# A two-layer transformer on one core: K and Q of layer 1 in one pass, the softmax division after P V, the row maximum fused

## The chip, the cores and the metric

The kernel runs on one core of a Trainium2 chip. The metric is the device time of one execution in microseconds. The core has five engines that run side by side and meet through semaphores: TensorE (PE in the profile, with PEld for its weight loads), VectorE (DVE), ScalarE (ACT), GpSimd (POOL) and SyncE (SP), which here issues all DMAs from a single queue. Each engine does its instructions in the order in which they were issued.

## The reference

Input is x of 2 batches x 512 positions x 512 features, in fp32. Two layers follow, each an attention and a feed-forward, each with a layer norm in front and a layer norm of its result before it is added to x:

```
x = x + LN(attention0(LN(x)))     32 heads of 128, 8 key/value heads, rotary, causal
x = x + LN(ffn0(LN(x)))           x W^T + bias, with 8 low-rank pairs
x = x + LN(attention1(LN(x)))     32 heads of 128, biases, not causal
x = x + LN(ffn1(LN(x)))           silu(h1) * h3 through 1376, with low-rank pairs
```

Attention of layer 1, which most of the change is about, is for each head

```
q = rmsnorm(x Wq + bq) * gq ;  k = rmsnorm(x Wk + bk) * gk ;  v = x Wv + bv
attn = softmax(q k^T / sqrt(128)) ;  out = concat(attn v) Wo + bo
```

## The kernel before, in words

All products are exact to about fp32: an operand is split into hi + lo[...], and `mm3` (line 393) issues hi hi, hi lo and lo hi. So every operand costs a cast to hi (often ScalarE) and a subtraction for lo (GpSimd or VectorE). `pick` (127) chooses for such an operation the engine that the planner expects to be done first.

The program is straight-line. A planner in Python lays out the order of issue: pieces of TensorE's work are `Item`s with a condition, and each has stages, written as generators, for the other engines and DMAs. `streams` (345) merges the main stream (scores and P V products) with fills (projections "q", V "v", output projections "o"), each placed at a nominal position in the main stream and let in when its condition holds. The planner keeps a clock of its own from a table of costs; `PHASES` (37) holds numbers of buffers and weights for six stages of the work. Large tiles share an arena of 37 slots of 128x1024 fp32 (`arena_t`, 230), where `NBUF` (171) limits each kind: in phases 3 and 4, which cover layer 1's attention, two "nat" tiles may live. What the planner decided is fixed: on the chip each engine follows that order and waits for what it needs.

A unit is a pair of heads of one batch; a layer has 32 units, in order, batch by batch for a few weights at a time. In layer 1, `l1_weights` (1020) loads K and Q weights of a pair in two halves each, split on the way, with two bias broadcasts. `proj` (1039) makes K, then Q: for 128 positions, 12 matmuls with x stationary and 256 weight columns moving. Two such results fill a PSUM bank (512 columns), then VectorE adds the bias into a tile "nat", ScalarE squares, VectorE sums, GpSimd raises to -1/2. K is multiplied by its row factors; Q's factors are kept for the softmax. `flip` (1097) transposes 32x32 blocks on VectorE, stores them to DRAM (kdk, kdq) and loads them back with the blocks in place, and splits them.

`l1_score` (1169) makes 128x512 scores in a bank (ps_s). VectorE takes the negated row maximum (`tensor_reduce`) and multiplies it by Q's row factor (mr); ScalarE's exp takes factor and maximum as scale and bias. `softmax_tail` (681), which layer 0 uses too, then divides: reciprocal of the row sum on VectorE, and a multiplication of P by `mul` on any of three engines. Layer 0's scores already have mask and maximum in one VectorE instruction (989).

In 110 of the 128 heads (flag "lag": 50 in layer 0, 60 in layer 1) P is transposed as K and Q are: blocks on VectorE (tile T), a store to pd or pc and four loads (PT), then the split into "pt" tiles. The P V products of such a head (`av_items`, 839) run during the next head: O^T accumulates in a bank ps_oy, ScalarE casts it to hi (with V's bias in layer 1), VectorE subtracts for lo, both from PSUM. `out_proj` (617) multiplies by Wo into ps_oy, and VectorE adds to y. The other 18 heads transpose P on TensorE (`pv_items`, 767).

Of the kernel before, what the change touches and what calls it, by code (L numbers as in the profile page):

```python
# [30 lines left out]
LAT = 0.1  # L31
FIRST = "x0 x1 x2 k x3 q r v y o z"
# [24 lines left out]
class Item:  # L57
    """a piece of TensorE's work, to be issued when cond holds"""
# [5 lines left out]
class Engine:  # L64
    """An engine that keeps its order of issue, with a clock (us) of its work."""
# [58 lines left out]
class Engines:  # L124
    WEIGHT = dict(vector=1.0, scalar=0.5, gpsimd=0.0)

    def pick(self, *cands):
        """issue the one of the candidates (engine, op, args...) that is done first"""
# [21 lines left out]
    def mul(self, out, a, s):  # L150
        """by a factor of each row"""
        self.pick(("gpsimd", "tensor_scalar", out, a, s, 1.0, ALU.mult, ALU.mult),
                  ("vector", "tensor_scalar", out, a, s, None, ALU.mult),
                  ("scalar", "activation", out, a, AF.Copy, dict(scale=s)))

    def copy(self, out, a):
        """from PSUM"""
        self.pick(("scalar", "copy", out, a), ("vector", "tensor_copy", out, a))
# [8 lines left out]
class Kern:  # L167
    """Work is written as items: functions, or generators that yield the time
    (of TensorE's work) after which their next stage is to be issued."""

    NBUF = dict(TN=1, KT=2, W=14, Wk=4, raw=3, bb=2, bqk=1, nat=2, qk=10, v=4, P=7, x=8, xn=2, pt=5, T=4, PT=3, ot=6, tmp=2, A=5,
                v32=2, q32=4, k32=3, p32=1,
                m=6, mr=6, rs=6, ri=6, st=6, mv=10, ve=8, r=10, c=8, r8=6, rq=4,
# [43 lines left out]
    # the large tiles: a half or the whole of a slot each (halves of one type only in a slot)  # L217
    HALF = dict(W=2, Wk=1, nat=2, v=2, PT=2, TN=2, KT=2, raw=1, bb=1, bqk=1, qk=1, P=1, x=1, A=1, T=1, xn=1, pt=1, ot=1,
# [77 lines left out]
    def phase(self, i):  # L296
        """what is tuned for each phase of the work"""
# [27 lines left out]
    def wait(self, tag, n=1):  # L325
        """in a stage: until n slots are free, first come first served"""
# [7 lines left out]
    def low(self, eng):  # L334
        """in a stage of low priority: until the engine has nothing issued to it"""
# [9 lines left out]
    def streams(self, main, fills, bg):  # L345
        """Issue the streams of items, each in its order: a fill when its nominal place in
        main has come, or main waits; bg starts at its nominal place."""
# [30 lines left out]
    def pe(self, t):  # L378
        """t: at the full clock, which TensorE has after a busy tick only"""
# [13 lines left out]
    def mm3(self, out, pairs, start=True, stop=True):  # L393
        """exact hi/lo products: hi hi + hi lo + lo hi"""
# [11 lines left out]
    def setup(self):  # L406
# [11 lines left out]
        self.pd = [self.dr.tile([P, 2, 4, 256], F32, name=f"pd{i}") for i in range(3)]  # L418
        self.kd = {n: [self.dr.tile([P, 4, 256], F32, name=f"kd{n}{i}") for i in range(2)] for n in "kq"}
        self.ready = {}  # L420
        self.ident = cp.tile([P, P], F32, name="ident")
# [7 lines left out]
    def consts(self):  # L429
# [5 lines left out]
        nc.vector.scalar_tensor_tensor(self.g, self.gqk[:, 0:1], SCALE, self.gqk[:, 1:2], ALU.mult, ALU.mult)  # L435
# [6 lines left out]
    def split(self, hi, lo, raw):  # L442
        """hi + lo = raw exactly"""
# [105 lines left out]
    def resid(self, b, tt, lvl):  # L549
        """x of level lvl + 1 = x + LN(y); returned short of a constant of each row"""  # L550
# [10 lines left out]
        if lvl == 3:  # L561
# [10 lines left out]
            nc.sync.dma_start(self.xsrc(b, tt, 4), x)  # L572
            self.rel(x)
# [6 lines left out]
        def store():  # L580
# [8 lines left out]
            nc.sync.dma_start(self.xsrc(b, tt, lvl + 1), xo)  # L589
            self.rel(xo)  # L590
# [3 lines left out]
    def boundary(self, b, tt, lvl):  # L594
        """from the finished y of level lvl on"""
# [21 lines left out]
    def out_proj(self, b, first, last, ot, w, badd, lvl):  # L617
        """y += O Wo over the heads of this unit"""
# [62 lines left out]
    def softmax_tail(self, st, j, qt, ps, bias, scale, w):  # L681
# [3 lines left out]
        rs = self.t("rs", [P, 1])  # L685
        nc.scalar.activation(pr[:, :w], ps[:, :w], AF.Exp, bias=bias, scale=scale, accum_out=rs)
        yield
        self.rel(bias, ps)
        ri = self.t("ri", [P, 1])
        nc.vector.reciprocal(ri, rs)  # L690
        yield
        nc.mul(pr[:, :w], pr[:, :w], ri)
        yield
        self.rel(rs, ri)
        if not st.get("lag"):
            st["p", j, qt] = pr
            return
        # P^T = 32 x 32 blocks transposed on VectorE, and the blocks put in place on their way through DRAM
# [19 lines left out]
        if ("T", j, qt ^ 1) not in st:  # L718
            return
        yield from self.wait("PT")  # L720
# [5 lines left out]
        for kc in ((1, 0), (0, 2, 3, 1))[h] if st["causal"] else range(NT):  # L726
# [21 lines left out]
            else:  # L748
                yield from self.wait("pt")
                hl = self.t("pt", [P, 2, 256], F32R)  # L750
                hi, lo = hl[:, 0, :], hl[:, 1, :]
            hi, lo = (x.rearrange(v, a=4, q=32) for x in (hi, lo))
# [6 lines left out]

    def unit_done(self, st):  # L760
        """after the last use of V"""
# [5 lines left out]
    def pv_items(self, st, j, voff, causal, bias):  # L767
        """transposes of P, then O^T = V^T P^T, split"""
        box = {}

        def tr(kc):
# [5 lines left out]
            if kc == NT - 1:  # L777
                self.rel(*[st["p", j, qt] for qt in range(NT)])
            n = S - q0 * P
# [59 lines left out]
    def av_items(self, st, j, voff, bias):  # L839
        """O^T = V^T P^T by halves of the queries, split"""  # L840
# [4 lines left out]
        def av(h, kc):  # L845
# [17 lines left out]
            if j == 1:  # L863
                self.unit_done(st)
            oh = self.t("ot", [P, S], F32R)
            ol = self.t("ot", [P, S], F32R)
# [816 lines left out]
```

## Time and profile before

| | |
|---|---|
| median of 3 runs | 2111.77 us (2107.32 to 2115.55) |
| the profiled execution: span, the only time that the page gives of it | 2117.8 us |
| TensorE busy | 2056.7 us, 97% |
| VectorE busy | 1801.4 us, 85% |
| GpSimd busy | 1446.3 us, 68% |
| ScalarE busy | 1337.7 us, 63% |
| DMA engines, mean busy share by the queue of SP | 60.9% |

The page gives the busy time of each engine, the granted clock of TensorE, and groups of instructions by operation and tile. Since every instruction goes through one helper, all have line 102, and a group is known by its tiles: ps_pj are projections, ps_s scores, ps_oy P V products and output projections, "ar" any tile of the arena. A matmul's own duration overlaps the next one's, so matmuls are timed by the pieces of a chain. Stages by time: start to about 700 us is layer 0's attention, its feed-forward runs between 640 and 800, layer 1's attention goes on to about 1890, and then comes layer 1's feed-forward. The median of the timed runs lies 6.0 us below the span of the profiled execution.

### The profile page before, as it was taken

The page shows a single profiled execution, that of the slowest core. Times are in us where ns is not written, and L with a number is a line of the kernel's source. Part 1 is how long each engine was busy: PE and PEld are TensorE (multiplying, and loading weights), DVE is VectorE, ACT ScalarE, POOL GpSimd, SP SyncE. Part 2 cuts the span into 40 slices and gives each one's busy share as a digit, 9 for nine tenths or more (in the row PEclk, how much of TensorE's full clock was granted, in tenths as well). Part 3 has the DMA queues.
Part 4 walks back from the last instruction along what each step waited for, and adds up shares of the span by engine and source line. Part 5 has one row for each costly group of instructions (what it writes and reads, how often), then busy time and mean ns, then how long its engine had stood idle before and what let it go on. Part 6 is the DMA issues. An engine that isn't in the chain of part 4 may idle for free.

```text
span 2117.8 us, 41211 instructions
## 1 busy us (share of the span) xinstructions
PE 2056.7 (97%) x12605; PEld 1827.5 (86%) x12605; DVE 1801.4 (85%) x4210; ACT 1337.7 (63%) x3247; POOL 1446.3 (68%) x1786
## 2 busy tenths in 40 slices
PE   8999999999999999999999999999999999989998
PEld 7888888888888798889899999999999898977886
DVE  7998899899888889889889999899989988888534
ACT  5776677577766668776666666666667666664212
POOL 5686678688875567877677777777777776774212
PEclk9999999999999999999999999999999999999999
DMA  2476567577652235887877777777777787763021
GB/s 98 127 183 166 145 185 183 143 200 199 177 159 66 71 103 166 244 232 223 227 202 229 220 227 211 207 221 219 225 206 232 213 240 212 224 178 93 31 67 44
DMA packets 476566, 370.54 MB, mean 175 GB/s; under 512 B 117400, under 2 KB 424488, under 8 KB 476344
## 3 DMA queue, kind: packets, MB, share of 16 engines
q1 hardware_dynamic: 476344, 367.91, 60.9%
q8 instruction: 99, 1.62, 0.3%
q14 instruction: 123, 1.01, 0.2%
HBM read 232.12 MB, written 135.66 MB: 174 GB/s over the span
## 4 chain that ended last, share of the span: by engine, by line
PE 54%; DMA 12%; DVE 9%; SPq 3%; issue 2%; POOL 2%; ACT 2%; DVEq 0%; ACTq 0%; POOLq 0%
PE ps_pj L102 23%; PE ps_oy L102 19%; PE ps_s L102 10%; DVE ar L102 6%; SPq L102 3%; DMA pd<-ar 3%; DMA ar<-pd 2%; POOL ar L102 2%; DMA kdk<-ar 2%; ACT ar L102 2%; DMA ar<-kdq 2%; DMA kdq<-ar 2%; PE ps_tr L102 1%; DMA ar<-pc 1%; DVE m L102 1%
## 5 line engine op out<-in xcount | busy, mean ns | idle before, releaser
L102 POOL TENSOR_TENSOR ar<-ar,ar 128x256 fp32r<-128x256 f32 (+4 forms) x1223 | 1058.3, 887 | 456.6 <-ACT ar L102 333.6
L102 PE MATMUL ps_oy<-ar,ar 128*128 128x256 f32 (+2 forms) x4014 | 832.2, 342 | 28.7 <-DVE ar L102 14.0
L102 PEld LDWEIGHTS ps_oy<-ar,ar 128*128 128x128 f32 x4014 | 653.5, 190 | 133.1 <-DVE ar L102 22.5
L102 ACT CAST ar<-ar 128x256 fp32r<-128x256 f32 (+3 forms) x1166 | 531.5, 490 | 305.4 <-DMA ar<-pd 117.1
L102 PE MATMUL ps_pj<-ar,xh 128*128 128x256 f32 (+1 forms) x3392 | 635.2, 285 | 0.9 <-POOL ar L102 0.6
L102 PEld LDWEIGHTS ps_pj<-ar,xh 128*128 128x128 f32 x3392 | 536.0, 190 | 14.5 <-POOL ar L102 1.1
L102 PE MATMUL ps_pj<-ar,xl 128*128 128x256 f32 (+1 forms) x1696 | 482.9, 285 | 0.0
L102 DVE STREAM_TRANSPOSE ar<-ar 128x256 f32<-128x256 f32 (+3 forms) x688 | 347.9, 533 | 16.9 <-DMA pd<-ar 9.7
L102 DVE TENSOR_TENSOR ar<-ps_pj,ar 128x512 f32<-128x512 f32 (+2 forms) x448 | 305.4, 683 | 52.5 <-PE ps_pj L102 44.8
L102 PE MATMUL ps_s<-ar,ar 128*128 128x512 f32 (+2 forms) x1252 | 338.5, 376 | 8.6 <-DVE ar L102 4.7
L102 PEld LDWEIGHTS ps_pj<-ar,xl 128*128 128x128 f32 x1696 | 322.9, 190 | 2.1 <-DVE xl L102 0.7
L102 PE MATMUL ps_pj<-xh,ar 128*128 128x512 f32 x816 | 286.6, 399 | 0.7 <-ACT xh L102 0.7
L102 DVE TENSOR_TENSOR y<-ps_oy,y 128x512 f32<-128x512 f32 x272 | 184.8, 680 | 81.8 <-PE ps_oy L102 80.2
L102 PEld LDWEIGHTS ps_s<-ar,ar 128*128 128x128 f32 x1252 | 214.5, 189 | 44.0 <-DVE ar L102 12.6
L102 DVE TENSOR_TENSOR ar<-ar,ar 128x256 fp32r<-128x256 f32 (+5 forms) x328 | 207.9, 652 | 51.1 <-ACT ar L102 50.1
L102 ACT ACTIVATE ar<-ps_s,mr,rq 128x512 f32<-128x512 f32 x256 | 198.6, 777 | 46.7 <-DVE mr L102 36.9
L102 PEld LDWEIGHTS ps_pj<-xh,ar 128*128 128x128 f32 x816 | 154.0, 189 | 31.7 <-ACT xh L102 1.1
L102 DVE TENSOR_REDUCE m<-ps_s 128x1 f32<-128x512 f32 x256 | 170.9, 673 | 6.2 <-PE ps_s L102 5.0
L102 ACT ACTIVATE ar<-ar,ri 128x512 f32<-128x512 f32 (+3 forms) x245 | 149.6, 621 | 38.3 <-DVE ri L102 37.1
L102 POOL TENSOR_SCALAR ar<-ar,ri 128x512 f32<-128x512 f32 (+3 forms) x202 | 133.0, 661 | 54.3 <-DVE ri L102 48.9
L102 PE MATMUL ps_pj<-xl,ar 128*128 128x512 f32 (+1 forms) x408 | 161.2, 395 | 0.0
L102 ACT ACTIVATE ar<-ps_s,m 128x512 f32<-128x512 f32 (+3 forms) x256 | 133.8, 526 | 23.4 <-DVE m L102 14.8
(91 smaller groups left out, 2105.5 us busy)
## 6 DMA issues: line engine op xcount, KB each, us to landing
pd<-ar SPq DMA_DIRECT2D x240, 256.0 KB, 3.7
ar<-pd SPq DMA_DIRECT2D x480, 128.0 KB, 3.3
ar<-pc SPq DMA_DIRECT2D x200, 128.0 KB, 3.0
ar<-in_wq SPq DMA_DIRECT2D x86, 256.0 KB, 4.1
ar<-in_wo SPq DMA_DIRECT2D x86, 256.0 KB, 3.6
kdk<-ar SPq DMA_DIRECT2D x31, 512.0 KB, 4.8
ar<-kdk SPq DMA_DIRECT2D x124, 128.0 KB, 4.0
kdq<-ar SPq DMA_DIRECT2D x31, 512.0 KB, 5.1
```

The costliest lines, as they stand in the source:

```text
L102: r = self.k.tc.keep_in_program_order(f(*args, **kw))
```

## The change

K and Q weights of a pair are laid side by side in one array, loaded in four quarters of 512 columns, and `proj` makes K and Q for 128 positions in one chain of 12 matmuls of 512 columns. Row factors are made per two positions' tiles, for K and Q together. Both nat tiles are taken at once. The projections of layer 1 get a nominal place half a head earlier (EARLY).

In heads with "lag" P is no longer divided. The row sums of the four query tiles gather in one 128x4 tile; `row_factors` takes its reciprocal, stores it to DRAM (rd) and loads it back as R, the 512 factors along the free axis in every partition. When O^T is complete, VectorE multiplies it by R from PSUM into a tile "ob", and the split reads that. A counter `turn` lets the transposes of layer 1's heads take their buffers in the order of heads.

In layer 1 the scores come negated (the factor g has the sign), and one `tensor_scalar` multiplies them by Q's row factor, in place in PSUM, and takes the row minimum; exp then has scale -1.

The rest of the diff: numbers of buffers for the new tiles, a planner stage between a store of x and the release of its tile, and comments taken out.

```diff
-                m=6, mr=6, rs=6, ri=6, st=6, mv=10, ve=8, r=10, c=8, r8=6, rq=4,
+                R=2, ob=1, rs4=3, ri4=2, v32=2, q32=4, k32=3, p32=1,
+                m=6, mr=6, rs=6, ri=6, st=6, mv=10, ve=8, r=10, c=8, r8=6, rq=8,
...
-        nc.vector.scalar_tensor_tensor(self.g, self.gqk[:, 0:1], SCALE, self.gqk[:, 1:2], ALU.mult, ALU.mult)
+        nc.vector.scalar_tensor_tensor(self.g, self.gqk[:, 0:1], -SCALE, self.gqk[:, 1:2], ALU.mult, ALU.mult)
...
@@ softmax_tail
+        if st.get("lag"):
+            if ("rs", j) not in st:
+                st["rs", j] = [self.t("rs4", [P, NT]), 0]
+            rs = st["rs", j][0]
+            nc.scalar.activation(pr[:, :w], ps[:, :w], AF.Exp, bias=bias, scale=scale, accum_out=rs[:, qt:qt + 1])
+            yield
+            self.rel(bias, ps)
+            st["rs", j][1] += 1
+            if st["rs", j][1] == NT:
+                self.spawn(lambda: self.row_factors(st, j, rs))
...
+        head = st["head", j]
+        while not st["causal"] and self.turn < head - 2:
+            yield 0.1
...
+        while not st["causal"] and self.turn < head:
+            yield 0.1
         yield from self.wait("PT")
...
+    def row_factors(self, st, j, rs):
+        nc = self.nc
+        ri = self.t("ri4", [P, NT])
+        nc.vector.reciprocal(ri, rs)
+        yield
+        self.rel(rs)
+        d = self.rd[st["slot", j]]
+        nc.sync.dma_start(d, ri)
+        yield
+        self.rel(ri)
+        yield from self.wait("R")
+        R = self.t("R", [P, S])
+        nc.sync.dma_start(R, d.rearrange("(o p) t -> o (p t)", o=1).broadcast_to([P, S]))
+        yield
+        st["R", j] = R
...
@@ av_items
+            yield from self.wait("ob")
+            t = self.t("ob", [P, S])
+            R = st["R", j]
+            nc.vector.tensor_tensor(t.rearrange("m (t p) -> m t p", t=NT), po.rearrange("m (t p) -> m t p", t=NT),
+                                    R.rearrange("m (p t) -> m t p", t=NT), ALU.mult)
...
-                nc.scalar.copy(oh, po)
-                yield
-                nc.vector.tensor_tensor(ol, po, oh.bitcast(F32), ALU.subtract)
+                nc.scalar.copy(oh, t)
+                yield
+                nc.sub(ol, t, oh.bitcast(F32))
...
@@ l1_weights
-        early = [bias] + [self.load_w(a["w" + n + "1"][hp], [P, NC, 256], w, n) for n in "kq"]
+        early = [bias] + [lambda c=c: quarter(c) for c in range(NC)]
...
@@ l1_pre
-            self.mm3(pj[:, z, :], [(self.xh[b][:, c, sl], self.xl[b][:, c, sl], w[n][0][:, c, :], w[n][1][:, c, :])
-                                   for c in range(NC)])
+            self.mm3(pj.rearrange("p n d -> p (n d)"),
+                     [(self.xh[b][:, c, sl], self.xl[b][:, c, sl], w["kq"][c // 2][0][:, c % 2, :], w["kq"][c // 2][1][:, c % 2, :])
+                      for c in range(NC)])
...
+            for i, n in enumerate("kq"):
+                nc.vector.tensor_tensor(st["nat" + n][:, tt, :], pj[:, i, :], w["b"][:, i * 256:i * 256 + 256], ALU.add)
...
-        early = [pq(1, "k", t) for t in range(4)] + [pq(0, "q", t) for t in range(4)]
+        early = [Item(lambda t=t: proj_ok(t), lambda t=t: proj(t)) for t in range(4)]
...
@@ l1_score
+            i = 4 + 2 * (qt % 2) + j
+            r = st["rq", qt // 2][:, i:i + 1]
             m = self.t("m", [P, 1])
-            nc.vector.tensor_reduce(m, ps, AX.X, ALU.max, negate=True)
-            yield
-            while "rq" not in st:
-                yield 0.3
-            r = st["rq"][:, 2 * qt + j:2 * qt + j + 1]
-            mr = self.t("mr", [P, 1])
-            nc.vector.tensor_tensor(mr, m, r, ALU.mult)
-            yield
-            self.rel(m)
-            yield from self.softmax_tail(st, j, qt, ps, mr, r, S)
+            nc.vector.tensor_scalar(ps, ps, r, 3.0e38, ALU.mult, ALU.min, accum_out=m)
+            yield
+            yield from self.softmax_tail(st, j, qt, ps, m, -1.0, S)
...
@@ run
-                    x.nom = x.nom or base + 2 + k * m / len(xs)
+                    x.nom = x.nom or base + 2 + k * m / len(xs) - (EARLY * m if L and f == "q" and len(xs) == 4 else 0)
```

## The prediction

> **What bounds the kernel now.** I read the page first, then a table of windows cut at the stages, then the chain of waits, then TensorE's own waits. The page gives each engine's share; the windows show where TensorE is not full. Columns: stretch in us, its length, busy us with number of instructions for PE, PEld, DVE, ACT, POOL, granted clock, DMA share, GB/s.
>
> ```profile
> PE 2056.7 (97%) x12605; PEld 1827.5 (86%) x12605; DVE 1801.4 (85%) x4210; ACT 1337.7 (63%) x3247; POOL 1446.3 (68%) x1786
> ...
> 860.00:1040.00 180.00, 172.65 (x1156) 156.94 (x1155) 159.04 (x344) 127.42 (x294) 138.26 (x164) 0.98 0.79 229
> 1040.00:1680.00 640.00, 634.97 (x4464) 589.14 (x4464) 583.40 (x1295) 416.28 (x961) 477.35 (x576) 1.00 0.76 220
> 1680.00:1880.00 200.00, 189.29 (x1269) 174.22 (x1268) 170.46 (x387) 129.56 (x291) 152.39 (x185) 0.97 0.79 225
> ```
>
> Layer 1's attention runs from about 700 to 1900 us. In its middle TensorE is busy 99% at full clock: it is the bound, and only less work for it shortens those 640 us. In the two shoulders it is busy 96 and 95% with a clock of 0.98 and 0.97; there something else is late now and then. VectorE (91% in the middle) is close behind, so work moved onto it counts. TensorE's waits over the whole span (total us, times, longest):
>
> ```profile
> PE ps_oy L102 <- DVE ar L102: 14.0, 17, 2.2
> ...
> PE ps_oy L102 <- POOL ar L102: 8.5, 14, 1.5
> PE ps_oy L102 <- ACT ar L102: 5.6, 7, 1.6
> PE ps_s L102 <- DVE ar L102: 4.7, 15, 0.5
> ```
>
> P V products and output projections (ps_oy) waiting for their SBUF operand are 28 us in 38 waits; scores (ps_s) waiting for Q and K 4.7 us, 4.5 of it in the middle in 14 waits. The time of a matmul must come from a chain, since matmuls overlap. Three pieces of the chain of waits (start, length, what):
>
> ```profile
> 1500.72 2.87 PE ps_pj L102 x24
> ...
> 1952.10 2.78 PE ps_oy L102 x12
> 1956.71 2.76 PE ps_s L102 x12
> ```
>
> 24 projections of 256 columns in 2.87 us are 120 ns each; 12 matmuls of 512 columns in 2.78 us are 231.5 ns each. I use these two pitches.
>
> **Part 1, one pass of 512 columns.** By the order of TensorE's instructions, 3072 projections of 256 columns become 1536 of 512. Each pair took 2 x 120 = 240 ns and its successor takes 231.5: 8.5 ns x 1536 = 13.0 us less, all of it on the engine that is the bound. A rule of the Trainium skill speaks against this: "TensorE: Matmul & The Clock Gate", section "Back-to-back issue gap", has a gap of N/2.4 + 2.5 ns, so a pair saves one fixed 2.5 ns: 3.8 us in all (an estimate from that page). The measured pitches are 11 ns (256) and 16 ns (512) above that formula's, so weight loads or issue cost more here than it allows; I take the row, 13.0, and keep 3.8 as the small end. What stands around it: bias additions become 256 of 128x256 from PSUM (the 415 ns row of the same shape) for 128 of 128x512 (683): +106 - 87 = +19 us on VectorE; squares likewise 256 x 402 - 128 x 630 = +22 us on ScalarE. Weights come in the same number and size of DMAs (84 for 84), one bias DMA fewer per set (-21). K and Q results now claim both "nat" buffers at once, where phases 3 and 4 allow two. That would hold a unit back if the previous unit still had them; the projections of a unit are spread over about one head (17 us), then come square, sum, factor, multiply and transposes (0.4 + 0.67 + 1.7 + 0.4 + 4 x 0.41, some 5 to 8 us with queueing), so the pair is held about 25 of the unit's 34 us. Cover 9 us; uncovered it would delay the projections of every unit. The planner's order keeps that rhythm: at the pitches above, the first score of a unit now stands some 29 us of TensorE work after its last projection, before 17 us. So the 4.5 us that scores waited for Q and K should go: I take -4, between 0 and -4.7.
>
> **Part 2, division moved to O^T** (110 heads, those that transpose P through DRAM). Removed: 440 reciprocals of 128x1 (146 ns: -64 us, VectorE), and 440 multiplications of P, until now spread over ScalarE (209: -132 us), GpSimd (170: -113) and VectorE (61: -39). Each lay between exp and transposition: 0.15 + 0.72 us less in the path of each P^T. Added: 110 reciprocals of 128x4 (about 0.15: +16), 110 multiplications PSUM by SBUF (680 ns, the row of ps_oy plus y: +75, VectorE), and the splits of O^T read SBUF: 60 on VectorE (818 for 731 ns: +5), 50 go to GpSimd or VectorE, whichever is free. On the DMA side, per head, a 2 KB store of factors in runs of 16 bytes and a 256 KB load that repeats one 2 KB row in all partitions. No row has either. For the load the nearest is the bias broadcast, 5.2 us to landing, against 3.3 for a P^T load; I take 5.2. For the store the bounds are the 2.4 us of the smallest P store and the 4.7 us of the bv load in 4-byte pieces; I take 3. Together, reciprocal 0.15 + 3 + 5.2 = 8.4 us after the last exp. It is needed only when the last P V product ends, and the first one stands 19 us of TensorE work after the last score, so 10 us of cover. If the cover were gone, the multiplication would stand at the head of VectorE's queue and hold all behind it (maxima, biases, transposes). The bytes: 110 x 0.26 = 29 MB on 370; in the middle about 7%, DMA share 0.76 to 0.81. SP issues 199 instructions more at 0.43 us each, 86 us; it must also wait for the store to land before it may issue the load, with all P^T loads behind it. In 74 of 110 heads three or more other DMAs stand between, which covers most of 3 us; in 36 there are two or fewer, some 1.5 us each. Against that stand 0.87 us gained in each P^T. The P^T path: exp 0.97, reciprocal 0.15, multiplication 0.72, transposition 0.70, store 3.7, four load issues 1.3, landing 3.3, cast 0.40, subtraction 0.77 = 12.0 us, of 19 available. Path value 0, between -15 (half of the 28 us of waits) and +44 (see the third rival).
>
> **Part 3, maximum fused.** 256 reductions (673) and 256 multiplications of 128x1 (365) go: -265 us. 256 tensor_scalar in place in PSUM with accumulation come; not in the trace, bounded by 673 (the reduction, which writes no row) and 837 (layer 0's fused mask and maximum, 700, with its accumulator read, 137). It is nearest to the latter: +214. The exp loses a per-row scale (777 to 686: -23 us on ScalarE). VectorE's part is off TensorE's path: value 0, and some 0.2 us less until a score bank is free.
>
> **Sum of the side engines.** VectorE: -265 + 214 - 64 + 16 + 75 - 39 + 19, and some 80 less for splits and casts that the planner sends elsewhere: about -120 of 1801. ScalarE: -132 + 22 - 23, and some 40 more for casts: about -95. GpSimd: multiplications -113 and 75 subtractions of 256 columns x 0.77, but 103 more of 512 columns x 1.31: about -50. No engine gets nearer to being the bound; SP and DMA do.
>
> **Sum on the path.** 2117.8 (span of the profiled execution; the page gives no other time of it) - 13.0 - 4 = 2100.8. The profiled execution lies 6.0 above the median of the runs, 2111.77, so 2094.8; I say 2095, -0.8%. Small ends: -3.8 alone gives 2108; -13 - 4.7 - 15 gives 2079.
>
> **Rivals.** *Given back as waits*: the matmuls shrink but the static order now meets DMAs that are 7% more, and TensorE waits for P^T as much longer. For it: in the middle ScalarE already waits 75.8 us for P^T loads. Against it: TensorE waits only 2.3 us there for ps_oy. The 13 come back as 3 to 13: 2102 to 2112, say 2107. *Shoulders fill*: where TensorE now waits, lighter VectorE, GpSimd and ScalarE bring P^T and O^T sooner. TensorE's waits away from both ends of the span are about 37 us, and the two shoulders lose 0.02 x 180 + 0.03 x 200 = 10 us to the clock; with 60% of that: 28 more, 2067. *Slower, the SP queue*: in the shoulders, where DMA share is 0.79 and TensorE waits for ps_oy some 20 times, P^T has no slack left. There are about 22 heads (380 us at 17). Each pays two issues (0.9) and the wait for the factors' landing (2.0, as SP's waits for a P store: 212.8 us in 105 times), less 0.87: 2.0 us; 44 in all, and TensorE at half clock after such gaps, some 4. 2117.8 - 17 + 48 - 6 = 2143. It decides once SP is late by more than the 19 - 12 = 7 us of slack that a P^T has, less what waiting for a turn costs it. For it: SP is already the chain's entry for 3% of the span, and the phases' buffer numbers are the same as before though R, ob and the nat pair want more room. That the change does not do what it says can be left out: the order of instructions shows all three parts.
>
> **How the numbers follow.** Forecast 0.50 (2087 to 2101 on its own), given back 0.15, shoulders fill 0.15, SP queue 0.20. What a measurement of this kernel tells from no change is 0.5%, below 2101.2 or above 2122.3. Faster: 0.15 + 0.47 of the forecast's 0.50 = 0.62; same: 0.15 + 0.03 = 0.18; slower 0.20. The range reaches down to the filled shoulders, 2066, and up into the rival with one third of its loss, 2126.
>
> **What would show it.** Part 1: pieces of 12 projections in 2.78 us where 24 stood in 2.87; PE busy less by 13. Scores: ps_s waiting for DVE near 0 in the middle. Part 2: VectorE waits for the R load near 0; SP's waits for the store of factors under 60 us; DMA share 0.81. Part 3: the new tensor_scalar near 700 ns. Wrong would be: a 512-column projection pitch above 240 ns; more than 40 us of ps_oy waits; a clock under 0.97 in the shoulders; projections waiting for weights at layer 1's start, since the first can't begin before all four quarters of K and Q are split.

## The result, and the profile after

The changed kernel takes 2199.41 us (median of four runs, 2198.13 to 2208.87) against 2111.78 for the kernel before on the same chip. The ratio is 1.043, 95% interval 1.040 to 1.045: 88 us slower, where 2095 was forecast. The profiled execution has a span of 2197.2 us (before 2117.8).

The page's first part:

```profile
span 2197.2 us, 38000 instructions
...
PE 2074.7 (94%) x11069; PEld 1758.6 (80%) x11069; DVE 1776.8 (81%) x3900; ACT 1259.1 (57%) x3235; POOL 1416.4 (64%) x1620
```

1536 matmuls are gone, every side engine has less to do, and the time is longer. Most of this is waiting: TensorE's idle time, the span less its busy time, grew from 61.1 to 122.5 us. The windows, with a stretch of layer 0 put first (columns as in the prediction):

```profile
100.00:580.00 480.00, 457.46 (x2439) 393.21 (x2439) 427.09 (x945) 269.79 (x812) 347.17 (x382) 0.99 0.74 187
860.00:1040.00 180.00, 168.42 (x906) 141.71 (x905) 145.47 (x314) 120.25 (x300) 135.48 (x146) 0.99 0.85 239
1040.00:1680.00 640.00, 613.60 (x3436) 527.35 (x3435) 521.90 (x1133) 389.20 (x982) 438.90 (x491) 0.99 0.82 226
1680.00:1880.00 200.00, 190.80 (x1048) 163.32 (x1047) 164.70 (x348) 123.53 (x314) 143.23 (x159) 0.97 0.83 233
```

The first row for the kernel before:

```profile
100.00:580.00 480.00, 474.59 (x2586) 413.92 (x2585) 428.70 (x1144) 332.66 (x960) 369.50 (x446) 1.00 0.66 176
```

TensorE did 2439 matmuls of layer 0 in the 480 us in which it did 2586 before: layer 0, which the forecast never looked at, loses too. In layer 1's middle TensorE is no longer full (613.6 of 640, before 635.0), and the DMA share is 0.82 where 0.81 was predicted. TensorE's waits and SP's (total us, times, longest), and the DMA issues (KB each, median us from issue to landing):

```profile
PE ps_s L103 <- POOL ar L103: 25.2, 29, 2.2
PE ps_oy L103 <- POOL ar L103: 20.5, 31, 2.0
...
PE ps_s L103 <- ACT ar L103: 15.5, 15, 3.0
PE ps_oy L103 <- DVE ar L103: 12.6, 14, 2.0
PE ps_oy L103 <- ACT ar L103: 11.5, 10, 6.1
```

```profile
SPq L103 <- DMA rd<-ri: 99.0, 54, 4.7
```

```profile
ar<-pd SPq DMA_DIRECT2D x480, 128.0 KB, 4.2
ar<-rd SPq DMA_DIRECT2D x110, 256.0 KB, 4.1
...
ar<-pc SPq DMA_DIRECT2D x200, 64.0 KB, 3.4
...
rd<-ri SPq DMA_DIRECT2D x110, 2.0 KB, 3.8
```

The same issues before:

```profile
ar<-pd SPq DMA_DIRECT2D x480, 128.0 KB, 3.3
...
ar<-pc SPq DMA_DIRECT2D x200, 64.0 KB, 2.3
```

Of the 79.4 us between the two spans, 61.4 are idle time of TensorE, and its waits account for it: they add up to 111.7 us, before 50.5. The other 18.0 are busy time, although TensorE has less to do. The mean granted clock is 0.984, before 0.993 (the trace has full and half clock, and 71 us at half clock, before 32); (1 - 0.984) x 2197 - (1 - 0.993) x 2118 = 20 us more lost to it. With 10 to 13 us of matmuls saved (below) that makes 7 to 10 of the 18; the remaining 8 to 11 us of busy time I can't name. Scores now wait for Q and K, 42 us in place of 8, and P V products and output projections 45 in place of 28. The loads of P^T shown land 0.9 and 1.1 us later than before; those of pc with 128 KB land 0.3 us later (3.0 to 3.3).

To place the loss I counted the matmuls that write ps_oy, a count that runs alike in all these kernels, and at four of them took the time minus the pitches of all matmuls up to there (120 ns for 256 columns, 231.5 for 512, others in proportion). What this excess is above that of the kernel before, in us:

| kernel | end of layer 0 (1400th) | layer 1 entered (1800th) | end of its middle (3400th) | attention's end (4000th) | time there |
|---|---|---|---|---|---|
| after | +32 | +38 | +74 | +92 | +79 |
| only_512_pass | -1 | +27 | +33 | +40 | +27 |
| only_division | +35 | +51 | +93 | +106 | +106 |
| p1_weights | -3 | +10 | +33 | +35 | +22 |
| p1w_e10 | -1 | +10 | +8 | +13 | 0 |
| cand_e10 | -1 | +8 | -8 | -4 | -17 |

Where part 1 is in, the last two columns differ by the 13 us that these pitches give it. That is put in, not measured; what was measured of it stands with part 1 below. The labels are those of the experiments.

### The profile page after: what moved, and what is told of

It is laid out like the page before. It is cut to its first block, busy times and chain, and to the rows that moved or that the text cites. A ratio compares the mean times of both kernels' runs of the same rounds, so it can differ in the third digit from the quotient of the medians.

```text
span 2197.2 us, 38000 instructions
## 1 busy us (share of the span) xinstructions
PE 2074.7 (94%) x11069; PEld 1758.6 (80%) x11069; DVE 1776.8 (81%) x3900; ACT 1259.1 (57%) x3235; POOL 1416.4 (64%) x1620
## 4 chain that ended last, share of the span: by engine, by line
PE 35%; DMA 15%; DVE 8%; POOL 4%; SPq 3%; issue 3%; ACT 2%; POOLq 0%; ACTq 0%; DVEq 0%
PE ps_pj L103 14%; PE ps_oy L103 12%; PE ps_s L103 7%; DVE ar L103 4%; POOL ar L103 4%; DMA pd<-ar 3%; SPq L103 3%; DMA ar<-kdk 2%; ACT ar L103 2%; DMA kdk<-ar 2%; DMA ar<-pd 2%; PE ps_tr L103 1%; DVE ps_s L103 1%; DMA rd<-ri 1%; DMA ar<-kdq 1%
## 5 line engine op out<-in xcount | busy, mean ns | idle before, releaser
L103 POOL TENSOR_TENSOR ar<-ar,ar 128x256 fp32r<-128x256 f32 (+3 forms) x1250 | 1150.2, 944 | 614.3 <-ACT ar L103 480.0
L103 PEld LDWEIGHTS ps_pj<-ar,xh 128*128 128x128 f32 x2368 | 401.4, 189 | 45.7 <-PE ps_tr L103 1.3
L103 DVE TENSOR_TENSOR ar<-ps_pj,ar 128x256 f32<-128x256 f32 (+3 forms) x576 | 314.4, 566 | 135.9 <-PE ps_pj L103 123.5
L103 ACT ACTIVATE ar<-ps_s,m 128x512 f32<-128x512 f32 (+3 forms) x512 | 309.3, 606 | 109.8 <-DVE ps_s L103 44.3
L103 DVE TENSOR_TENSOR ar<-ar,ar 128x256 fp32r<-128x256 f32 (+4 forms) x273 | 202.9, 754 | 75.3 <-ACT ar L103 71.4
L103 PEld LDWEIGHTS ps_pj<-ar,xl 128*128 128x128 f32 x1184 | 224.3, 189 | 25.8 <-DVE xl L103 2.3
L103 DVE TENSOR_SCALAR_CACHE_REDUCE ps_s<-ps_s,rq 128x512 f32<-128x512 f32 x256 | 188.1, 741 | 18.6 <-PE ps_s L103 16.6
L103 DVE TENSOR_TENSOR ar<-ps_oy,ar 128x512 f32<-128x512 f32 (+1 forms) x124 | 126.2, 1018 | 2.1 <-PE ps_oy L103 1.6
L103 DVE CUSTOM_DVE_ANT_0 ps_s<-ps_s,ar 128x512 f32<-128x512 f32 (+3 forms) x256 | 122.0, 492 | 6.9 <-PE ps_s L103 6.9
L103 ACT ACTIVATE ar<-ar 128x256 f32<-128x256 f32 (+1 forms) x272 | 102.5, 421 | 30.1 <-DVE ar L103 19.3
```

Source lines behind the costliest of these rows:

```text
L103: r = self.k.tc.keep_in_program_order(f(*args, **kw))
```

## The experiments

All ratios are to the kernel before on the same chip, with 95% intervals.

### Each part alone

*only_512_pass* takes the projections of K and Q, their weights, their bias and the constant EARLY from the changed kernel, and nothing else:

```diff
-        early = [bias] + [self.load_w(a["w" + n + "1"][hp], [P, NC, 256], w, n) for n in "kq"]
+        early = [bias] + [lambda c=c: quarter(c) for c in range(NC)]
...
+            self.mm3(pj.rearrange("p n d -> p (n d)"), ...)
```

> The kernel before with the first part alone: K and Q in one pass of 512 columns, both nat tiles at once, EARLY. Theory S (the moved division, with its trip of the factors through the DMA queue, carries the loss): TensorE has 13 us less, nothing else is late: 2095 to 2103. Theory N (K and Q come late, since both share one chain and claim both nat buffers: scores wait): 2125 to 2150, with over 15 us of ps_s waits for POOL and ACT in the middle of layer 1.

*only_division* takes the moved division, with the order of turns that belongs to it (softmax_tail, row_factors, av_items, pv_items):

```diff
+            if st["rs", j][1] == NT:
+                self.spawn(lambda: self.row_factors(st, j, rs))
```

> The kernel before with the division moved to O^T alone. Theory S: most of the 88 us: 2180 to 2200, with layer 0 some 30 us longer. Theory N: only layer 0's 30 us and little more: 2135 to 2150.

*only_max* takes the fused maximum:

```diff
-            nc.vector.tensor_reduce(m, ps, AX.X, ALU.max, negate=True)
+            nc.vector.tensor_scalar(ps, ps, r, 3.0e38, ALU.mult, ALU.min, accum_out=m)
```

> The kernel before with the maximum of layer 1 fused with the row factor alone. Both theories: 2105 to 2113, VectorE 50 us less busy and nothing on the path.

*no_division* is the changed kernel with the division put back on P (parts 1 and 3 together):

```diff
-            if st["rs", j][1] == NT:
-                self.spawn(lambda: self.row_factors(st, j, rs))
+        nc.vector.reciprocal(ri, rs)
+        nc.mul(pr[:, :w], pr[:, :w], ri)
```

> The changed kernel with the division back where it was (multiplication of P, no factors through DRAM): parts one and three together. Theory S: 2090 to 2103, faster than before. Theory N: 2125 to 2155.

| kernel | median us | ratio | interval |
|---|---|---|---|
| only_512_pass | 2142.48 | 1.017 | 1.015 to 1.018 |
| only_division | 2215.49 | 1.050 | 1.048 to 1.052 |
| only_max | 2120.54 | 1.006 | 1.004 to 1.007 |
| no_division | 2159.09 | 1.024 | 1.021 to 1.026 |

No part gains, and three of the four lie above every range that was expected of them: only_division, only_max by a little, and no_division. The division is the large part: 0.050 x 2112 = 106 us alone, some 41 us on top of the other two parts (1.043 less 1.024). The three sum to 154 us, and together they cost 88; why they overlap so much was not traced. The 512 pass loses most of what it loses at the entry of layer 1 (table above), and TensorE falls out of full clock there. The window from 740 us on, before (the one that follows it stands in the prediction):

```profile
740.00:860.00 120.00, 115.63 (x784) 104.51 (x783) 102.14 (x232) 83.62 (x171) 80.61 (x111) 1.00 0.48 145
```

and both in only_512_pass:

```profile
740.00:860.00 120.00, 106.10 (x546) 86.35 (x545) 94.47 (x218) 72.86 (x153) 64.82 (x86) 0.95 0.37 114
860.00:1040.00 180.00, 169.50 (x888) 144.20 (x888) 147.21 (x340) 130.32 (x309) 138.85 (x152) 0.95 0.78 228
```

### What a new order alone costs

Every edit of this kernel makes the planner write another order. *planner_latency* changes nothing but one of its constants:

```diff
-LAT = 0.1
+LAT = 0.12
```

> The kernel before, with the planner's constant for the delay between engines at 0.12 us rather than 0.10: the same work, in a somewhat other order. If the order of before is an ordinary one, 2100 to 2116. Theory T (the buffers and weights of the phases fit that very order, and any other costs time): 2118 to 2140, as the fused maximum alone, 2120.5, hints.

2119.02 us, ratio 1.004 (1.003 to 1.005). So only_max's 0.6% is about what another order costs by itself. This is one other order, and it cost what its second expectation said; with it as the measure, a difference of half a per cent between kernels with different orders proves nothing of the part that was edited.

### The division, taken apart

*div_contiguous* reads R along its rows, where only_division reads it with a step of four elements. The factors then stand in a wrong order within a head:

```diff
-                                    R.rearrange("m (p t) -> m t p", t=NT), ALU.mult)
+                                    R.rearrange("m (t p) -> m t p", t=NT), ALU.mult)
```

> The moved division alone, with R read along its rows instead of every fourth element, the order of every instruction the same (the factors reach the wrong queries: this leaves their order out). Theory S1 (the trip through SP and DMA makes P^T late): the multiplication falls from 1061 to about 690 ns, the time stays at 2200 to 2216. Theory S2 (the slow multiplication at the head of VectorE's queue): 2150 to 2180.

2217.05 us, 1.050 (1.048 to 1.053). The multiplication took 674 ns in place of 1070, and the time stayed:

```profile
L102 DVE TENSOR_TENSOR ar<-ps_oy,ar 128x512 f32<-128x512 f32 x110 | 74.2, 674 | 4.5 <-ACT ar L102 2.0 <-PE ps_oy L102 1.8 <-DMA pc<-ar 0.4
```

*div_no_trip* leaves out the store of the factors and the load of R and multiplies by a constant tile of ones, so the division is left out:

```diff
-        nc.sync.dma_start(d, ri)
-        nc.sync.dma_start(R, d.rearrange("(o p) t -> o (p t)", o=1).broadcast_to([P, S]))
+        st["R", j] = self.Rc
```

> The moved division alone, with a constant tile of ones in place of R: no store, no load, no wait for them (the division is left out). Theory S1: 2100 to 2130. Theory S2: 2185 to 2215, for the multiplication and all of VectorE's work is still there.

2136.73 us, 1.011 (1.009 to 1.014): some 80 us of the 106 go with the trip of the factors through DRAM. This kernel's order is another one too; the kernels below, with one order, put 99 us on the trip. *div_no_multiply* keeps the trip and splits O^T from PSUM as the kernel before, without the multiplication:

```diff
-            nc.vector.tensor_tensor(t.rearrange("m (t p) -> m t p", t=NT), po..., R..., ALU.mult)
-                nc.scalar.copy(oh, t)
+                nc.scalar.copy(oh, po)
```

> The moved division alone, with the factors stored and loaded, but no multiplication: O^T is split from PSUM as before (the division is left out). Theory S1: 2180 to 2215. Theory S2: 2105 to 2135, since P is not multiplied either and VectorE has 115 us less.

2257.69 us, 1.068 (1.064 to 1.073), slower still than with the multiplication. So taking the multiplication away brought nothing back. The order without it is worse than only_division's, for reasons I did not trace; that the multiplication's length costs no time rests on div_contiguous, which keeps the order.

### What of the trip costs: the bytes, the stand, the issues or the order

The trip does four things at once. First two kernels on bytes and stand. *trip_small* loads four factors into each partition where R had 512:

```diff
-        nc.sync.dma_start(R, d.rearrange("(o p) t -> o (p t)", o=1).broadcast_to([P, S]))
+        nc.sync.dma_start(R[:, :NT], d[0:1, :].broadcast_to([P, NT]))
```

> The kernel of only_division with the same 11457 TensorE instructions in the same order on every queue, and one thing changed: the load of R brings 2 KB (four factors on each of the 128 partitions) and no longer 256 KB, so 28 MB less go through the DMA engines; the store, both issues on SP's queue and the wait of the load for the store stay. Left out of the computation: each block of 128 queries is multiplied by the factor of its first query. Theory B (the bytes and the packets of R crowd the DMA engines, every other landing is late): most of the 80 us between only_division and div_no_trip come back, 2135 to 2165, and the loads of P^T land in 3.3 to 3.8 us again. Theory Q (SP's queue: two more issues per head and the stand until the store has landed): 2195 to 2220, as only_division, with SP's waits for ri's store still over 80 us.

*trip_late* delays both issues in the planner's time, with nothing left out:

```diff
+        yield 0.5
         nc.sync.dma_start(d, ri)
         yield
+        yield 2.5
```

> The whole computation of only_division; the planner lets 0.5 us pass before it issues the store of the row factors and 2.5 us more before the load of R, so that other issues go between the two on SP's queue. Theory Q (SP stands until the store has landed): SP's waits for the store fall from 93 us to under 40 and the time from 2215 to 2150 to 2185. Theory B (bytes): 2205 to 2225. A third possibility: R comes too late for the multiplication and holds the bank, 2220 or more with more waits of ps_oy.

trip_small: 2181.18 us, 1.031 (1.029 to 1.034). That lies between the two expectations: the bytes are a large part, 40 us. trip_late: 2254.18 us, 1.066 (1.063 to 1.068), although SP's stand is gone:

```profile
SPq L102 <- DMA rd<-ri: 5.7, 7, 1.6
```

It was 93.3 us in only_division. So the stand, which I had thought the chief cost, either costs little or was replaced; as trip_late's order differs, it cannot say which. The next kernels keep the order of only_division on every engine. *trip_order* charges the planner for both transfers and issues neither (R is a constant tile of ones):

```diff
-        nc.sync.dma_start(d, ri)
+        self.ghost(d)
...
-        nc.sync.dma_start(R, ...)
+        self.ghost(R)
```

> The order of only_division on every engine, with the store of the row factors and the load of R not issued (R is a constant tile of ones, so the division is left out). Theory Q (what is left of the trip's cost beside its bytes is the two issues per head and SP's stand for the store): 2130 to 2145, as div_no_trip. Theory O (it is the order that the planner writes once R's arrival is a condition, with one 2 KB half of an arena tile held by R): 2170 to 2190, as trip_small.

*trip_no_stand* is trip_small with the small load taken from an input, so that it waits for no store:

```diff
-        nc.sync.dma_start(R[:, :NT], d[0:1, :].broadcast_to([P, NT]))
+        nc.sync.dma_start(R[:, :NT], self.a["lA"][0:1, :NT].broadcast_to([P, NT]))
```

> trip_small in the same order with both issues kept, but the small load takes its four numbers from an input in place of the stored factors, so it needn't wait for the store to land (each query block is multiplied by a constant, so the division is left out). If SP's stand for the store is the cost of the remaining half: 2135 to 2155. If it is the number of issues alone or the order: 2170 to 2185, as trip_small with 2181.

*trip_store_only* is trip_order with the stores issued:

```diff
-        self.ghost(d)
+        nc.sync.dma_start(d, ri)
```

> trip_order with the 110 stores of the row factors issued, and no load of R (the division is left out, R is a constant tile of ones). If each added issue on SP's queue costs alike: half of the 55 us between trip_order and trip_no_stand, 2145 to 2157. If the store is what costs, since it stands on SP's queue for the last reciprocal of the head with the loads of P^T behind it: 2160 to 2182. If the load is what costs: 2120 to 2135.

These five kernels issue their work in one and the same order on every engine (the constant tile is one memset more at the start), so each step of this ladder adds one transfer or one wait. One other thing varies: the multiplication takes 674 ns in trip_small and trip_no_stand, where its factor is one value repeated, and 1070 in the other three. By div_contiguous, which differs from only_division in this length alone, that costs no time (1.0503 and 1.0501).

| step | kernel | median us | ratio | interval | step, x 2112 us |
|---|---|---|---|---|---|
| order and engine work only | trip_order | 2123.12 | 1.0032 | 1.0018 to 1.0045 | +7 |
| + 110 stores of 2 KB | trip_store_only | 2168.78 | 1.0257 | 1.0232 to 1.0281 | +48 |
| + 110 loads of 2 KB that wait for nothing | trip_no_stand | 2179.43 | 1.0291 | 1.0273 to 1.0310 | +7 |
| + their wait for the store | trip_small | 2181.18 | 1.0310 | 1.0285 to 1.0335 | +4 |
| + 28 MB more in those loads | only_division | 2215.49 | 1.0501 | 1.0480 to 1.0523 | +40 |

At each of the two small steps the intervals overlap; at the two large ones they lie far apart. A store of 2 KB per head costs about as much as 256 KB of load per head, and a load of 2 KB next to nothing. The traces on either side of the two large steps. Windows of layer 0 and layer 1's middle, the DMA queue (packets, MB, share of 16 engines' span), issues, the largest of TensorE's waits and two of SP's in trip_order:

```profile
100.00:580.00 480.00, 473.65 (x2576) 412.87 (x2575) 447.10 (x1003) 283.23 (x856) 366.97 (x405) 1.00 0.66 174
1040.00:1680.00 640.00, 633.56 (x4437) 588.83 (x4437) 572.27 (x1120) 422.82 (x968) 408.41 (x502) 1.00 0.77 218
```

```profile
q1 hardware_dynamic: 476344, 367.91, 61.9%
...
pd<-ar SPq DMA_DIRECT2D x240, 256.0 KB, 3.2
ar<-pd SPq DMA_DIRECT2D x480, 128.0 KB, 4.0
```

```profile
PE ps_oy L102 <- POOL ar L102: 19.4, 36, 2.0
```

```profile
SPq L102 <- DMA pc<-ar: 33.0, 30, 2.9
...
SPq L102 <- DMA pd<-ar: 24.3, 26, 5.3
```

trip_store_only:

```profile
100.00:580.00 480.00, 469.07 (x2521) 405.10 (x2520) 440.66 (x982) 279.77 (x843) 363.30 (x399) 1.00 0.68 171
1040.00:1680.00 640.00, 625.66 (x4361) 578.51 (x4360) 561.66 (x1102) 413.76 (x954) 398.23 (x488) 1.00 0.80 214
```

```profile
q1 hardware_dynamic: 492184, 368.15, 63.3%
...
pd<-ar SPq DMA_DIRECT2D x240, 256.0 KB, 3.7
ar<-pd SPq DMA_DIRECT2D x480, 128.0 KB, 4.4
```

```profile
PE ps_oy L102 <- POOL ar L102: 31.8, 58, 2.0
```

```profile
SPq L102 <- DMA pc<-ar: 58.4, 43, 3.8
SPq L102 <- DMA pd<-ar: 38.7, 38, 4.7
```

trip_small and then only_division, the queue alone:

```profile
q1 hardware_dynamic: 508024, 368.38, 62.7%
```

```profile
q1 hardware_dynamic: 508024, 396.99, 66.8%
```

0.24 MB of stores raise the DMA share in the middle from 0.77 to 0.80. In engine time over the whole span that is 0.633 x 16 x 2158.7 - 0.619 x 16 x 2126.6 = 801 us, 7.3 for each store. But the store's own packets are not what fills it. By the packet records of the trace its 128 pieces of 16 bytes took 9 ns each, 130 us for all 110 stores, and about 30 us more went into packets of 4 bytes; 550 of the 801 us are other transfers' packets of 1 KB that took longer (67 ns in place of 62). With R it is different. From trip_small to only_division the same working gives 1832 us, and R's own packets of 2 KB account for it (2026 us, less the 114 of the small load).

What the store does shows in the landing of other transfers. The order of issue is the same in all five kernels, so each DMA can be compared with itself. The times are mean us from issue to landing, where all five traces tell it:

| transfer | trip_order | trip_store_only | trip_no_stand | trip_small | only_division |
|---|---|---|---|---|---|
| store of P, issued right behind the factors' store (73) | 3.03 | 3.88 | 4.00 | 4.04 | 3.97 |
| store of P, more than 6 issues behind it and R's load (104) | 3.37 | 3.55 | 3.65 | 3.74 | 3.88 |
| load of P^T, 1 to 4 issues behind R's load (243) | 3.27 | 3.44 | 3.36 | 3.29 | 4.26 |

The factors' store makes the store of P behind it land 0.85 us later, and others some 0.2. SP, which waits for P's stores before it issues the loads of P^T, stands 40 us longer for them (its two lines above). The split of P^T (GpSimd's) comes later, and P V products wait for it 12 us longer. That each of these follows from the one before is read from two traces, not tested. R's 256 KB make the loads of P^T behind them land 1.0 us later; the small load, in pieces of 16 bytes like the store, delays nothing that I can see. In each case the time is lost in many small pieces over layers 0 and 1 alike: at the 1400th ps_oy matmul trip_store_only is 11 us behind trip_order, at the 4000th 33 (these two executions are 32 us apart, the medians 46).

The Trainium skill has a rule for small pieces ("DMA: Bandwidth & Descriptors", section "Specifications"): transfers below 512 bytes don't reach the line rate, as the engine reads, modifies and writes. No run here shows that this is the store's cost: its packets took 9 ns, and loads in pieces of the same size cost 7 us.

Two things stay open. One is why a store lands later behind the factors' store. The other is how the 48 us divide between that and the store's place on SP's queue, where it waits for the head's last reciprocal (15.2 us of SP's waits, against 3.4 for ri in trip_order) with other issues behind it; no run stores the factors without that wait.

### The 512 pass, taken apart

*p1_weights* asks for the K and Q weights of layer 1's first four pairs three units ahead, in only_512_pass two:

```diff
-... ((2, 0), (2, 1), (0, 0)))
+... ((3, 0), (2, 1), (0, 0)))
```

> The kernel of only_512_pass with the K and Q weights of layer 1's first four pairs asked for three units ahead instead of two. Theory W (the loss of 27 us at the entry to layer 1 comes from weights that are split too late, since all four quarters have to be ready before the first projection): 2115 to 2128. Theory N (it comes from the longer time that the nat pair and the first scores stand apart, and from ScalarE's and VectorE's load there): 2137 to 2148.

*p1_early0* takes the constant back that places a pair's projections half a head ahead:

```diff
-EARLY = 0.5
+EARLY = 0.0
```

> The kernel of only_512_pass with the projections of a pair placed as before (EARLY = 0 in place of 0.5: not half a head ahead). Theory W: 2138 to 2150, the entry is lost as before. Theory N: the pair nat is held for a shorter time, 2120 to 2135. If the early placing is what makes the flips ready in time in the middle of layer 1, 2155 or more, with new waits of ps_s there.

p1_weights: 2142.4 us, 1.013 (1.010 to 1.015). By the table the entry improves from +27 to +10, as the theory of late weights has it, but most of the gain is lost again in the middle (+10 to +33), where scores wait for the splits of K and Q:

```profile
PE ps_s L103 <- POOL ar L103: 12.3, 15, 1.9
PE ps_s L103 <- ACT ar L103: 5.6, 5, 1.4
```

p1_early0: 2212.74 us, 1.046 (1.043 to 1.049), and the loss grows through all of layer 1. So the place of the projections is worth far more than their width. *p1w_e075* and *p1w_e10* move them on, with the earlier weights kept:

```diff
-EARLY = 0.5
+EARLY = 0.75     (p1w_e10: 1.0)
```

> p1_weights with the projections of a pair placed three quarters of a head ahead (EARLY 0.75, before 0.5). If the scores' waits for the split of K and Q are what the 512 pass still loses in the middle of layer 1, 2110 to 2132; if the loss comes from another place, 2137 to 2150.

> p1_weights with the projections of a pair placed a whole head ahead (EARLY 1.0). By the same two theories 2105 to 2130 or 2137 to 2155; a pair of nat tiles is then held longer, and if arena space runs out for it, slower than with 0.75.

2124.57 us, 1.004 (1.003 to 1.005), and 2119.05 us, 1.001 (1.000 to 1.002). In layer 1's middle the list of p1w_e10's waits has no score any more. By the table it still loses 10 us at the entry and 3 more after it, which equals the 13 that part 1 is put at. *cand_e10* adds the fused maximum to it (the changed kernel without the moved division, weights three units ahead, EARLY 1.0):

```diff
-LEAD = (... ((2, 0), (2, 1), (0, 0)))
-EARLY = 0.5
+LEAD = (... ((3, 0), (2, 1), (0, 0)))
+EARLY = 1.0
```

> Parts 1 and 3 without the moved division, with the weights of layer 1's first four pairs asked for three units ahead and the projections a whole head ahead (p1w_e10 with the fused maximum). 1536 matmuls less at 13 us in sum; p1w_e10 was level with the kernel before. If the fused maximum frees the scores' bank earlier by some 0.2 us on each of 256 tiles and nothing gives it back: 2095 to 2110, faster than both. If the order written for the tuned kernel gives it back, as in only_max: 2110 to 2130.

2106.99 us, 0.997 (0.995 to 0.998): 4.4% faster than the changed kernel (0.9966 / 1.0427), and 0.3% below the kernel before. Its page and its middle:

```profile
span 2101.2 us, 38204 instructions
...
PE 2039.1 (97%) x11069; PEld 1751.3 (83%) x11069; DVE 1690.5 (80%) x4199; ACT 1386.2 (66%) x3481; POOL 1444.6 (69%) x1735
```

```profile
1040.00:1680.00 640.00, 639.86 (x3664) 559.99 (x3664) 520.32 (x1308) 469.24 (x1147) 487.37 (x564) 1.00 0.76 225
```

TensorE is busy for 639.9 of 640 us, in the same stretch of the kernel before for 635.0. The interval excludes no gain at all, but 0.3% is below the 0.5% that the prediction set as its bound, and no more than planner_latency's other order moved the time. So it is not shown that the parts themselves made it.

## Why the prediction was wrong

**Part 1's matmuls: right.** "8.5 ns x 1536 = 13.0 us less". In the changed kernel's chain of waits twelve 512-column projections take:

```profile
1196.55 2.78 PE ps_pj L103 x12
...
1202.14 2.80 PE ps_pj L103 x12
```

that is 232 to 233 ns each, where 231.5 was taken. Over all successive projections of the two traces, start to start and without those over 1.15 times the median, the mean is 118.8 ns (256 columns, before) and 231.0 (512, after): 6.6 ns a pair, 10 us. So the step is right and its size some 3 us too large. The rule that gives 3.8 is, on its page, that of a matmul by itself; in these chains both pitches lie above it.

**Part 1's surroundings: wrong.** "So the 4.5 us that scores waited for Q and K should go: I take -4." They went, and waits for GpSimd's and ScalarE's splits took their place (9.2 and 3.5 us in the middle of only_512_pass, 42 in all of the changed kernel). Larger is the entry of layer 1. The prediction named the cause as a thing that would make it wrong, weights that must all be split before the first projection, but put no price on it. It is 27 us, of which 17 came back with earlier weights. That the pair of nat tiles has 9 us of cover was not tested by itself.

**Part 2, the step that failed: "Path value 0, between -15 and +44".** It costs 106 us alone. Four of its terms were off. (1) The store was given "3 us", a latency on R's own way, and nothing for what it does to the transfers behind it: it costs 48 us. (2) The load's bytes were turned into a DMA share (0.76 to 0.81, measured 0.85 in only_division and 0.82 in after), and the share was then given no price: 40 us. A share of 0.81 was no sign of room; each P^T's way holds a store and a load, and the medians of both rose (3.2 to 4.2 and 4.0 to 4.9 us from trip_order to only_division). (3) The slack of a P^T, 7 us (19 - 12), was taken as one figure, and from layer 1. The 38 waits of ps_oy, 28 us, that the prediction lists itself are pieces (P V products and output projections) that had no slack even before; any delay adds to such waits (85 us in only_division). And layer 0, which holds 50 of the 110 heads, lost 35 of the 106. (4) The multiplication was costed at 680 ns and took 1061, but div_contiguous shows that this costs no time.

**The rival "slower, the SP queue"** had the right sign, the wrong mechanism and a third of the price (31 us of 88). It rested on SP's stand for the landing of the factors' store (2.0 us a head, in 22 heads). SP does stand, 99 us in all, above the "under 60" of the prediction, but between trip_no_stand and trip_small the stand is worth 4 us, within the noise. The waits of SP that grew with the store are those for P's own stores (40 us more), which no rival named. The limit to the shoulders was wrong as well: the loss runs through both layers.

**Part 3** was near: 741 + 138 = 879 ns for the fused instruction with its accumulator read, 837 taken. Its value alone is 0 as forecast, as far as can be told (only_max lies near what a new order costs). Beside the repaired part 1 the ratio went from 1.0008 to 0.9966; that may be score banks that come free earlier, or the order again, and is not shown. The sum for VectorE was far off, -120 us where its busy time fell by 25; 42 us of that are the slower multiplication.

**The forecast's argument as a whole** leaned on TensorE being the bound. In this kernel some pieces came late already before (the 28 us of ps_oy's waits), so whatever lands later adds to the time, and a late piece also costs clock: 20 us of the 79 are granted clock. The rival "given back as waits" had this way of losing time, but gave it 3 to 13 us. Of the signs that it set itself, "more than 40 us of ps_oy waits" came (45) and "DMA share 0.81" nearly (0.82). The upper end of its range, 2126, fits a third of the SP queue's 44 us on top of the time before; with the 17 us gained, as in its other sums, it would be 2111.

## What to carry to other kernels

Don't price a transfer by its bytes alone: here 2 KB of store, once a head on a busy queue, cost about as much time as 256 KB of load, and 2 KB of load next to nothing. Before a transfer is called hidden, list what is issued right behind it in every stage and what slack that has, piece by piece and not on average. Read what a transfer costs from the landing of the others, not from the DMA share alone. And where a planner writes the order, test a cause with kernels whose order is the same and which differ in one transfer: those five ratios settled what re-planned variants had left in doubt.

## What the runs showed of the hardware

VectorE's product of a PSUM operand with an SBUF operand of 128x512 took 674 ns where the SBUF operand was read along its rows and 1061 to 1073 where each element lay 16 bytes after the last. The Trainium skill states a line of 16 bytes in SBUF and a penalty for each access that leaves it ("SBUF — State Buffer", section "Door 1: The DMA port swizzle"), which fits; only these two steps were measured. Where the operand was one value repeated 128 times (trip_small) it took 674 ns too.

The factors' store (2 KB, issued by SP among other DMAs) took 3.8 to 4.2 us to land by the median, and the store issued right behind it landed 0.85 us later than without it. A load of 2 KB in the same number of 16-byte pieces took 3.0 to 3.5 us and delayed nothing that the traces show. In both directions the packets of 16 bytes took 9 ns.
